# First mixer of an eight-layer stack: four moves of work and of loads around its filters

## Chip, cores and metric

The kernel runs on one core of a Trainium2 chip. The metric is device time in microseconds (us) of one execution.

## The reference

The reference is a stack of four mixers and four feed-forward layers, each as `x = x + layernorm(layer(layernorm(x)))`, on 8 sequences of 512 tokens with 256 channels in float32. Only the first mixer is touched:

```python
q, k, v = short_conv(x @ W.T, conv)                 # each with silu
beta = sigmoid(x @ Wb.T)
A = where(strictly_lower, -(kb @ k.T), 0)           # per chunk of 32 tokens; kb = k * beta
T = inverse(eye - A); u = T @ v; w = T @ kb
S, o: u_adj = u - w @ S; o = q @ S + attn @ u_adj; S = S + k.T @ u_adj     # chunk by chunk
local_s, local_m, local_l = fir(v, 3 / 15 / 63 taps)
p = softmax(gate logits)                            # five gates per head
o = p0*local_s + p1*local_m + p2*local_l + p3*delta + p4*v
out = rmsnorm(o) @ Wo.T
```

## The kernel before

`l0_attn` (from line 275) works in three stages. Instructions are written in Python order, but that is only a priority: a planner puts every instruction on its engine's list at build time, by a model of its own, and takes the first in Python order whose inputs and buffers it believes to be ready. On the chip each list then runs strictly in order, with semaphore waits. The SyncE queue (SP) issues nearly all loads and stores, ScalarE's queue (ACTq) a few stores.

**Front**, per block b of 512 tokens, 0 to 7 (`front`, lines 434 to 511): normalise and transpose x (L133 on VectorE, L146 on TensorE), project to k, q, v (L448), convolve over four taps (L454 on ScalarE, L456 on VectorE), silu (L459), transpose v into the resident tile `Vw` (L486, L488), and form the products k·k of 64-token chunks (L499, L502), stored to DRAM as `s_d` (L505, L509).

`strengths(g, p)` (L372) turns the rows of four blocks into beta over the squared norm of k and writes them to `g_d`: two loads of rows (L377), a tanh (L381), four small VectorE instructions (L382 to L386), four stores (L388). It runs after block 3 for group 0 and after block 7 for group 1, with its tiles in the front's pool.

`inverse(g)` (L328) is a generator for the chunk inverses of four blocks. It works in the residual's own tiles, `K.XA`, which are loaded again later (`K.load_x`, L74). Its first step loads 2 MB of products (L331) and the strengths (L333). Then come some 60 VectorE instructions in the tile (L343 to L357). Its tail is an `affine_select` and a small copy on GpSimd (L360, L363), one store of 2 MB (`t_d`, L364), and four ScalarE copies of 128x1024 (L367), each followed by a 512 KB store (`tt_d`, L368) and sharing two buffers `tt`. One step of `inverse(0)` is taken at each step of the front from block 4 on, tail included.

**Filters**, 32 groups g of 8 channels (`filters`, L617): TensorE multiplies `Vw` with a Toeplitz tile (L627, two PSUM tiles per group, six PSUM buffers). Three Toeplitz tiles exist, two of them in `K.XA[4:8]`; each is loaded afresh for its next group (L544, L547). VectorE multiplies by the gates (L632, two buffers `pr`) and adds the four terms (L638 into `s1`, L640 into `s2`, two buffers); ACTq stores the result to `f_d` (L642). `gates(h)` (L566 to L585) makes the gates of head h from `rw_all` (loaded by L553). `scaled_v` (L612) and `query_scales` (L590 to L599) prepare operands of the third stage. The filters' pools `fa`, `fb` reuse the memory of the front's pools.

**Back**, per block (`back`, L725): loads (`loads`, L695 to L720: `load_tt` L401, L699, L702, L705, L712 to L720), chunk products from L735 on, sequential state, residual sum (L182). Before it stand `inverse(1)`'s first step and `load_x` of blocks 0 to 3. The loop takes one step of `inverse(1)` at every second step, drains it when block 3 has begun, and then loads block 4.

Of the kernel before, what the change touches and what calls it, by code (L numbers as in the profile page):

```python
# [14 lines left out]
ALU = mybir.AluOpType  # L15
# [259 lines left out]
def l0_attn(K):  # L275
    nc, tc = K.nc, K.tc
# [4 lines left out]
    HALF = NB // 2  # L281
    with ExitStack() as es:
        def pool(stack, name, bufs, **kw):
            return stack.enter_context(tc.tile_pool(name="l0" + name, bufs=bufs, **kw))
# [15 lines left out]
        def window(t, offset, *ap):  # L300
            a = t[0:1, 0:1]
            return bass.AP(tensor=a.tensor, offset=a.offset + offset, ap=[list(x) for x in ap])
# [25 lines left out]
        def inverse(g):  # L328
            flat = K.XA[:, HALF * g:HALF * g + HALF].rearrange("p b n d -> p (b n d)")
            T = flat.rearrange("p (i j) -> p i j", i=64)  # L330
            nc.sync.dma_start(out=flat, in_=s_d[g * P:(g + 1) * P, :])  # L331
            gb = pin.tile([P, 64], F32, tag="gb", name=f"gb{g}")
            nc.sync.dma_start(  # L333
                out=gb, in_=window(g_d, g * P * 64, (64, P), (1, 64)))
            gn = pin.tile([P, 64], F32, tag="gn", name=f"gn{g}")
            nc.vector.tensor_scalar(gn, gb, -1.0, None, ALU.mult)
            yield

            def blocks(t, at, *ap):
                return bass.AP(tensor=t.tensor, offset=t.offset + at,  # L340
                               ap=[list(t.ap[0])] + [list(x) for x in ap])
            both = blocks(flat, 0, (2080, 2), (64, 32), (1, 32))
            nc.vector.tensor_tensor(  # L343
                both, both, blocks(gn, 0, (32, 2), (1, 32), (0, 32)), ALU.mult)
            yield
            for j in range(1, 31):
                r = 31 - j
                tmp = pin.tile([P, 512], F32, tag="tmp", name=f"tmp{g}_{j}")
                tmp = tmp[:, 0:2 * r * j].rearrange("p (q a b) -> p q a b", q=2, a=r)
                low = blocks(flat, 64 * (j + 1), (2080, 2), (64, r), (1, j))  # L350
                nc.vector.tensor_tensor(
                    tmp, blocks(flat, 64 * (j + 1) + j, (2080, 2), (64, r), (0, j)),
                    blocks(flat, 64 * j, (2080, 2), (0, r), (1, j)), ALU.mult)
                nc.vector.tensor_tensor(low, low, tmp, ALU.add)
                if j % 2:
                    yield
            nc.vector.tensor_tensor(  # L357
                both, both, blocks(gb, 0, (32, 2), (0, 32), (1, 32)), ALU.mult)
            yield
            nc.gpsimd.affine_select(  # L360
                out=T, in_=T, compare_op=ALU.is_gt, fill=0.0, base=0,
                pattern=[[1, 64], [-1, 64]], channel_multiplier=0)
            nc.gpsimd.tensor_copy(flat[:, 0:4096:65], gb)  # L363
            nc.sync.dma_start(out=t_d[g * P:(g + 1) * P, :], in_=flat)  # L364
            for q in range(4):
                tt = pin.tile([P, 16, 64], F32, tag="tt", name=f"tt{g}_{q}", bufs=2)
                nc.scalar.copy(tt, T[:, :, 16 * q:16 * q + 16].rearrange("p i j -> p j i"))  # L367
                nc.scalar.dma_start(  # L368
                    out=tt_d[g * P:(g + 1) * P, 1024 * q:1024 * q + 1024],
                    in_=tt.rearrange("p i j -> p (i j)"))  # L370
            yield

        def strengths(g, p):

            rw = p.tile([32, 2, 4, 64], F32, tag="rws", name=f"rws{g}")
            for m, at in enumerate((0, 28)):
                nc.sync.dma_start(  # L377
                    out=rw[:, m].rearrange("p h t -> p (h t)"),
                    in_=rows_d[32 * g:32 * g + 32, at * 64:at * 64 + 256])
            bt = p.tile([32, 256], F32, tag="bts", name=f"bts{g}")  # L380
            nc.scalar.activation(bt, rw[:, 0].rearrange("p h t -> p (h t)"), AF.Tanh, scale=0.5)  # L381
            nc.vector.tensor_scalar(bt, bt, 0.5, 0.5, ALU.mult, ALU.add)  # L382
            den = rw[:, 1].rearrange("p h t -> p (h t)")
            nc.vector.tensor_scalar(den, den, 1e-6, None, ALU.add)
            nc.vector.reciprocal(den, den)
            nc.vector.tensor_tensor(bt, bt, den, ALU.mult)  # L386
            for b in range(HALF):
                nc.sync.dma_start(  # L388
                    out=window(g_d, (HALF * g + b) * 2048, (256, NT), (1024, 2), (1, 256)),
                    in_=bt[J * b:J * b + J, :])  # L390
# [15 lines left out]
        with ExitStack() as e1:  # L406
            pv = pool(e1, "v", 1)
            Vw = pv.tile([P, NB, J, D], F32, name="Vw")
            with ExitStack() as ef:
                p1, p2, p3 = pool(ef, "a", 1), pool(ef, "b", 2), pool(ef, "d", 3)  # L410
# [100 lines left out]
                        in_=S[64:128, :, :, 0:64])  # L511

                inv = iter(())
                for b in range(NB):
                    for _ in front(b):
                        next(inv, None)
                    if b % HALF == HALF - 1:
                        strengths(b // HALF, p1)
                    if b == HALF - 1:
                        inv = inverse(0)  # L520
                        next(inv)

            with ExitStack() as ef:
                p1, p2 = pool(ef, "fa", 1), pool(ef, "fb", 2)
# [93 lines left out]
                def filters(g):  # L618

                    h = g // 8  # L620
                    pr = p2.tile([P, 4, 4, 64], F32, tag="pr", name=f"pr{g}")
                    for half in range(2):
                        ps = pmm.tile([P, 2, 4, 64], F32, tag="fir", name=f"pf{g}_{half}")
                        for m in range(2):
                            for r in range(2):
                                c = 4 * r + 2 * half + m
                                nc.tensor.matmul(  # L627
                                    ps[64 * r:64 * r + 64, m],
                                    lhsT=Vw[:, :, :, 8 * g + c].rearrange("p b j -> p (b j)"),
                                    rhs=toep[g % NB_T][:, :, :, c],  # L630
                                    start=True, stop=True)
                        nc.vector.tensor_tensor(  # L632
                            pr[:, 2 * half:2 * half + 2], ps[:, :, :, ::-1],
                            gt[:, h, None].to_broadcast([P, 2, 4, 64]), ALU.mult)
                    if g + NB_T < G:
                        load_toep(g + NB_T)
                    s1 = p1.tile([P, 4, 2, 64], F32, tag="s1", name=f"s1_{g}")
                    nc.vector.tensor_tensor(s1, pr[:, :, 0:2, :], pr[:, :, 2:4, :], ALU.add)  # L638
                    s2 = p2.tile([P, 4, 64], F32, tag="s2", name=f"s2_{g}")
                    nc.vector.tensor_tensor(s2, s1[:, :, 0, :], s1[:, :, 1, :], ALU.add)  # L640
                    for r in range(2):
                        nc.scalar.dma_start(  # L642
                            out=f_d[:, (8 * g + 4 * r) * 64:(8 * g + 4 * r + 4) * 64],
                            in_=s2[64 * r:64 * r + 64].rearrange("p c t -> p (c t)"))

                gates(0)
                given = False
                for g in range(G):
                    filters(g)
                    if g % 8 == 4 and g < 24:  # L650
                        gates(g // 8 + 1)
                    if g == 2:
                        value_scales()
                    if g == 22:
                        query_scales()
                    if g % 4 == 3:
                        scaled_v(g // 4)
                    if next(inv, 0) == 0 and not given:
                        given = True
                        for b in range(2):  # L660
                            load_tt(b)
        assert given
        inv = inverse(1)
        next(inv)
        K.load_x(K.i["x"], range(HALF))


        p1, p2 = pool(es, "ba", 1), pool(es, "bb", 2)
# [203 lines left out]
        K.log_exp_tables()  # L872
        K.log_exp = True
        ahead = {b: loads(b) for b in range(2)}
        live, done, begun, steps = [back(0, *ahead[0])], 0, 1, 0
        while live:
            for x in list(live):
# [188 lines left out]
class Choice:  # L1066
# [7 lines left out]
    E, NL, K = 48, 10, 128  # L1074
# [1556 lines left out]
```

## Time and profile before

| | |
|---|---|
| time, median of 3 runs | 4565.85 us (4554.68 to 4568.97) |
| profiled execution: time; span | 4579.0 us; 4577.3 us |
| TensorE / VectorE / ScalarE / GpSimd busy | 87% / 59% / 43% / 45% |
| first mixer in the span | 0 to about 705 us |
| its filters, TensorE continuously | 278.50 to 387.45 us |
| mean granted TensorE clock over the span | 0.925 |

The span runs from the first to the last instruction; the profiled time is 1.7 us more. A line of the timeline gives start, duration, engine, source line, operation, tile written <- tile read, shapes and count; in brackets stand the idle time before it and what ended that. A line of the waits gives the waiting instruction <- the one waited for: total us, times, longest. A row of a table by stage gives the stretch, its length, the busy time (and instructions) of TensorE, its weight loads, VectorE, ScalarE and GpSimd, then the granted TensorE clock as a share of full speed, the share of the 16 DMA engines, and GB/s.

### The profile page before, as it was taken

How to read it: one execution, taken by the hardware profiler on the slowest of the kernel's cores; microseconds unless marked ns; L12 is line 12 of the kernel's file. 1: busy time of each engine (PE TensorE's matmuls, PEld its weight loads, DVE VectorE, ACT ScalarE, POOL GpSimd, SP SyncE). 2: the span in 40 equal slices, each digit the busy share in tenths (PEclk: the TensorE clock that was granted, in tenths of full speed). 3: DMA queues.
4: the chain of work that ended last, by engine and by line, in shares of the span. 5: the costliest groups of instructions: out<-in, count | busy, mean ns of one | idle time of the engine just before them, and what ended most of it. 6: DMA issues, size and time to landing. Idle time of an engine off the chain costs nothing. (4 is left out here: it accounts for less than half of the span.)

```text
span 4577.3 us, 63200 instructions
## 1 busy us (share of the span) xinstructions
PE 3989.2 (87%) x21672; PEld 2642.3 (58%) x21672; DVE 2710.9 (59%) x7215; ACT 1982.9 (43%) x4082; POOL 2043.3 (45%) x2013
## 2 busy tenths in 40 slices
PE   8887898999998599789999978898988866899997
PEld 3435675555555399644454544565655544678884
DVE  7677656456647611255566534888888899721115
ACT  5511433444344233334444444767676655311112
POOL 0000322444344234345555423889888879223321
PEclk9897998999999799889999989999999986899999
DMA  4467621000000199500000002344333434236653
GB/s 117 142 180 193 174 50 45 18 10 6 7 5 20 52 249 251 148 5 10 6 6 6 1 23 67 122 125 127 124 123 121 125 106 138 93 121 230 228 182 113
DMA packets 389361, 442.89 MB, mean 97 GB/s; under 512 B 147469, under 2 KB 271487, under 8 KB 388527
## 3 DMA queue, kind: packets, MB, share of 16 engines
q1 hardware_dynamic: 361087, 390.18, 28.4%
q0 software_dynamic: 16272, 31.87, 2.6%
q10 hardware_dynamic: 11680, 16.80, 1.1%
q8 instruction: 172, 2.82, 0.3%
q14 instruction: 150, 1.23, 0.1%
HBM read 372.49 MB, written 66.26 MB: 96 GB/s over the span
## 5 line engine op out<-in xcount | busy, mean ns | idle before, releaser
L2046 POOL TENSOR_TENSOR h<-h,C 128x1024 f32<-128x1024 f32 x256 | 613.5, 2409 | 137.6 <-DVE h L2042 95.0
L2042 DVE TENSOR_TENSOR_SCAN h<-dA,dB 128x512 f32<-128x512 f32 x480 | 568.1, 1208 | 91.0 <-ACT dA L2030 77.3
L1000 POOL TENSOR_SCALAR p<-p,rs 128x128 f32<-128x128 f32 (+3 forms) x256 | 275.9, 1085 | 416.5 <-DVE rs L999 260.5
L2030 ACT ACTIVATE dA<-dl,A 128x512 f32<-128x512 f32 x480 | 330.5, 690 | 174.4 <-DVE h L2042 173.6
L1566 DVE CUSTOM_DVE_ANT_0 junk<-S,mask 128x256 f32<-128x256 f32 (+3 forms) x512 | 249.5, 487 | 195.1 <-PE S L1560 156.8
L2059 PE MATMUL y<-C,h 128*128 128x128 f32 x2048 | 295.3, 295 | 73.0 <-POOL h L2046 72.8
L2059 PEld LDWEIGHTS y<-C,h 128*128 128x128 f32 x2048 | 260.2, 153 | 158.5 <-POOL h L2046 102.9
L1594 ACT ACTIVATE PT<-T 128x128 f32<-128x128 f32 (+3 forms) x512 | 198.1, 435 | 278.9 <-PE T L1589 267.9
L1560 PE MATMUL S<-KZ,QT 64*128 64x512 f32 (+3 forms) x1024 | 260.1, 491 | 23.8 <-DVE mx L1566 23.6
L2258 PE MATMUL gb<-xbT,w_b 128*128 128x256 f32 (+1 forms) x1472 | 255.3, 332 | 1.0 <-ACT ts L2462 0.6
L2258 PEld LDWEIGHTS gb<-xbT,w_b 128*128 128x128 f32 x1472 | 230.2, 191 | 23.1 <-ACT ts L2462 0.8
L2264 DVE TENSOR_TENSOR hTb<-sb,gb 128x512 f32<-128x512 f32 x71 | 48.8, 687 | 325.4 <-PE gb L2258 314.1
L2025 POOL TENSOR_TENSOR dB<-du,B 128x1024 f32<-128x1024 f32 x96 | 233.8, 2436 | 0.1
L1844 PE MATMUL pf<-fT,w_l_ffn 128*128 128x512 f32 x384 | 206.6, 676 | 28.5 <-ACT fT L1838 11.3
L1589 PE MATMUL T<-QT,KZ 64*128 64x384 f32 (+3 forms) x1024 | 217.1, 465 | 2.9 <-ACT PT L1594 2.5
L2025 DVE TENSOR_TENSOR dB<-du,pb 128x1024 f32<-128x1024 f32 x160 | 191.2, 1195 | 23.4 <-ACT pb L2023 21.3
L182 POOL TENSOR_TENSOR X<-X,yn 128x256 f32<-128x256 f32 (+1 forms) x56 | 79.7, 1441 | 263.0 <-ACT yn L177 233.1
L1334 ACT ACTIVATE hT<-h,w_l_ffn 128x128 f32<-128x128 f32 x384 | 109.5, 368 | 198.0 <-PE h L1329 198.0
L1329 PE MATMUL h<-xgT,w 128*128 128x128 f32 x1536 | 185.1, 279 | 0.0
L1560 PEld LDWEIGHTS S<-KZ,QT 64*128 64x128 f32 x1024 | 116.7, 193 | 114.0 <-issue 58.3
L1597 POOL TENSOR_SCALAR_AFFINE_SELECT PT<-PT 128x512 f32<-128x512 f32 x128 | 81.3, 635 | 219.1 <-ACT PT L1594 206.2
L998 ACT ACTIVATE p<-p,nm 128x128 f32<-128x128 f32 (+3 forms) x256 | 143.5, 561 | 80.7 <-DVE nm L994 72.7
(587 smaller groups left out, 9147.0 us busy)
## 6 DMA issues: line engine op xcount, KB each, us to landing
w_b<-l3f_w SPq DMA_DIRECT2D x138, 512.0 KB
C<-xdd SPq DMA_DIRECT2D x256, 256.0 KB
B<-xdd SPq DMA_DIRECT2D x256, 256.0 KB
w<-l1f_w SPq DMA_DIRECT2D x48, 1024.0 KB
w<-l1f_w SPq DMA_DIRECT2D x48, 256.0 KB
X<-x SPq DMA_DIRECT2D x16, 512.0 KB
c<-ys SPq DMA_DIRECT2D x16, 512.0 KB
X<-l0fd SPq DMA_DIRECT2D x22, 320.0 KB
```

Source lines behind the costliest of these rows:

```text
L1000: nc.gpsimd.tensor_scalar(p[:, 0:n], p[:, 0:n], rs, None, ALU.mult)
L1560: nc.tensor.matmul(ps[:, 0:n], lhsT=QT[half, qt * P:n], rhs=KZ[half, j % 2, 0:n], start=True, stop=True)
L1566: nc.vector.tensor_tensor_reduce(out=junk[:, 0:n], in0=ps[:, 0:n], in1=mask[:, L - n:L], scale=1.0, scalar=-3.0e38, op0=ALU.add, op1=ALU.m ...
L1589: nc.tensor.matmul(ps[:, 0:n], lhsT=KZ[half, j % 2, kt * P:(kt + 1) * P], rhs=QT[half, kt * P:L], start=True, stop=True)
L1594: nc.scalar.activation(PT[:, j, :], ps[:, 0:n], AF.Exp)
L1844: nc.tensor.matmul(ps, lhsT=gu[:, k, j * 768 + c * P:j * 768 + (c + 1) * P], rhs=R[b]["fT"][:, k, :], start=(k == 0), stop=(k == 1))
L2025: on.tensor_tensor(dBs[k], R[b]["du", h], B[:, None, :].to_broadcast([P, 2, L]), ALU.mult)
L2030: nc.scalar.activation(dA, R[b]["dl", h][:, c, :], AF.Exp, scale=A[:, 2 * h + c, n:n + 1])
L2042: nc.vector.tensor_tensor_scan(hs[k][:, c, :], dA, dBs[k][:, c, :], 0.0, ALU.mult, ALU.add)
L2046: nc.gpsimd.tensor_tensor(hs[k], hs[k], row_C.pop(k)[:, None, :].to_broadcast([P, 2, L]), ALU.mult)
L2059: nc.tensor.matmul(R[b]["y", h][q // 2][:, q % 2, c * P:(c + 1) * P], lhsT=t[:, c, q * P:(q + 1) * P], rhs=K.ident, is_transpose=True, sta ...
L2258: nc.tensor.matmul(ps[:, q, :], lhsT=ww[:, k, (c + q) * P:(c + q + 1) * P], rhs=xT[:, k, :], start=(k == 0), stop=(k == 1))
```

## The change

It has four parts. The tail of `inverse(0)` is no longer stepped during the front: the step in front of it now yields `True`, at which the front stops stepping, and the tail is written after filter group 1, followed by `load_tt` of blocks 0 and 1. `strengths(1)` moves from the end of the front to filter group 21, with its tiles in the filters' pool. The two sums of the filters go from VectorE to GpSimd. And `load_x` of blocks 0 to 3 and the first step of `inverse(1)` are written after the loads of back blocks 0 and 1 instead of ahead of them, `load_x` first.

```diff
@@ inverse
             nc.vector.tensor_tensor(
                 both, both, blocks(gb, 0, (32, 2), (0, 32), (1, 32)), ALU.mult)
-            yield
+            yield True
             nc.gpsimd.affine_select(
@@ the loop over the front
                 inv = iter(())
+                inverted = True
                 for b in range(NB):
                     for _ in front(b):
-                        next(inv, None)
-                    if b % HALF == HALF - 1:
-                        strengths(b // HALF, p1)
+                        inverted = inverted or next(inv)
                     if b == HALF - 1:
+                        strengths(0, p1)
                         inv = inverse(0)
-                        next(inv)
+                        inverted = next(inv)
+                assert inverted
@@ filters
-                    nc.vector.tensor_tensor(s1, pr[:, :, 0:2, :], pr[:, :, 2:4, :], ALU.add)
+                    nc.gpsimd.tensor_tensor(s1, pr[:, :, 0:2, :], pr[:, :, 2:4, :], ALU.add)
                     s2 = p2.tile([P, 4, 64], F32, tag="s2", name=f"s2_{g}")
-                    nc.vector.tensor_tensor(s2, s1[:, :, 0, :], s1[:, :, 1, :], ALU.add)
+                    nc.gpsimd.tensor_tensor(s2, s1[:, :, 0, :], s1[:, :, 1, :], ALU.add)
@@ the loop over the filters
                 gates(0)
-                given = False
                 for g in range(G):
                     filters(g)
...
                     if g % 4 == 3:
                         scaled_v(g // 4)
-                    if next(inv, 0) == 0 and not given:
-                        given = True
+                    if g == 1:
+                        for _ in inv:
+                            pass
                         for b in range(2):
                             load_tt(b)
-        assert given
-        inv = inverse(1)
-        next(inv)
-        K.load_x(K.i["x"], range(HALF))
+                    if g == 21:
+                        strengths(1, p1)
@@ the back
         ahead = {b: loads(b) for b in range(2)}
+        K.load_x(K.i["x"], range(HALF))
+        inv = inverse(1)
+        next(inv)
         live, done, begun, steps = [back(0, *ahead[0])], 0, 1, 0
```

## The prediction, made before the changed kernel was run

> **What bounds the stage now.** The change touches only the first mixer, some 705 us of the span, so I cut that into stages and asked in each what TensorE waits for. First the table by stage: front blocks 4, 5, 6 and 7, the hand-over to the filters, the filters, the hand-over to the back.
>
> ```profile
> 122.67:147.97 25.30, 23.64 (x97) 11.19 (x97) 21.04 (x35) 15.53 (x30) 2.01 (x2) 1.00 0.63 183
> 147.97:182.42 34.45, 27.53 (x98) 13.88 (x97) 32.64 (x61) 15.97 (x29) 0.20 (x1) 0.80 0.23 57
> 182.42:220.53 38.11, 27.25 (x97) 13.84 (x97) 22.10 (x43) 23.07 (x32) 6.45 (x4) 0.84 0.51 172
> 220.53:248.84 28.31, 26.36 (x97) 12.00 (x96) 13.32 (x20) 16.73 (x30) 0.00 (x0) 0.91 0.62 159
> 248.84:278.50 29.66, 11.69 (x49) 4.95 (x49) 21.04 (x44) 2.31 (x4) 1.80 (x1) 0.74 0.87 227
> 278.50:387.45 108.95, 108.42 (x464) 47.05 (x464) 83.83 (x163) 0.94 (x2) 0.00 (x0) 0.98 0.65 194
> 387.45:402.69 15.24, 0.00 (x0) 0.03 (x1) 8.73 (x17) 1.28 (x1) 4.27 (x11) 0.57 0.78 229
> ```
>
> An undisturbed block takes 25.30 us with TensorE busy for 23.64. Block 5 is long by VectorE, which carries the inverse (32.64 of 34.45). Block 6 is longer still, 38.11, though VectorE has only 22.10: something else. The filters are TensorE's (108.42 of 108.95). Both hand-overs leave TensorE idle, 17.97 and 15.24 us. The timeline of ScalarE in block 6 and the waits of that stretch say why:
>
> ```profile
> 213.73 1.91 ACT L367 COPY tt<-X 128x1024 f32<-128x1024 f32 x1 [2.81 <-DMA l0tt<-tt]
> 215.55 0.58 ACT L488 COPY Vw<-pvw 128x512 f32<-128x512 f32 x1
> ...
> 216.04 1.95 ACT L367 COPY tt<-X 128x1024 f32<-128x1024 f32 x1
> 217.90 0.57 ACT L488 COPY Vw<-pvw 128x512 f32<-128x512 f32 x1
> ```
>
> ```profile
> DVE ca L456 <- ACT ca L454: 22.7, 1, 22.7
> ```
>
> The inverse's copies sit between the front's own, one of them waiting for a store to free its buffer, and VectorE starves for 22.7 us. Then the waits of the first hand-over, of SP at the second, and of the back:
>
> ```profile
> POOL toep L536 <- DMA l0g<-bts: 44.4, 1, 44.4
> ...
> PE pf L627 <- DVE rw_all L567: 9.8, 1, 9.8
> ...
> PE pf L627 <- DVE pr L632: 8.1, 1, 8.1
> DVE rky L90 <- DMA l0g<-bts: 5.6, 1, 5.6
> ```
>
> ```profile
> SPq L702 <- DMA l0v<-vs: 8.4, 1, 8.4
> ```
>
> ```profile
> PE pW L735 <- DMA TS<-l0t: 15.3, 1, 15.3
> ```
>
> The filters' pool opens only when the second strengths are stored (their tile is in memory that it reuses); TensorE then waits for the gates. At the other end the first back block waits for its load L702, and that for memory that the last store of `vs` still reads.
>
> **Part 1, the tail held.** In block 4 the last convolution instruction ends at 142.44 + 1.52 = 143.96, and the next block's first transpose starts at 147.97, 4.0 us later. In block 6 it ends at 201.43 + 4.02 = 205.45, and the next starts at 220.53: 15.1 us, 11.1 more. The next block's transposes to projections take 225.90 - 220.53 = 5.4 us instead of 151.42 - 147.97 = 3.5, another 1.9. At most 13.0 us go. But I don't expect the copies to wait for the filters: the list takes whatever is ready. The Toeplitz tile's memset ran at 126.91, and three residual loads, written after all filters, at 218.02. So the tail keeps its time and only loses its rank: the four copies (4 x 1.95 = 7.8 us) become fillers in ScalarE's gaps. One gap of 3.48 us per block is free; the others are about 1 us, and a copy started there delays the front by up to 1. I charge 5 of 7.8: gain 8.0, from 13.0 - 7.8 = 5.2 to 13.0 if order alone decides, and zero if the copies keep their place. Next late is TensorE itself (23.64 of 25.30). With the copies move GpSimd's 4.07 + 0.37 us (L360, L363), a 2 MB store on SP, four of 512 KB on ACTq, and behind them the `load_tt` and residual loads that wait for it. If all that were held until group 1, GpSimd's 4.4 us would stand ahead of the sums, 1.2 groups of 3.76 us, against three groups of PSUM; the transfers are rival S.
>
> The trace shows that slow clock: eight transposes took 1.97 us after the stall against 1.09 in other blocks, at a granted 0.91 for the block. [...]
>
> **Part 2, strengths at group 21.** The pool now waits for the last store of products, issued until 251.55, instead of the last store of strengths, issued until 255.76: 4.2 us. The strengths store landed 1.5 to 1.7 us after issue; the products' store is larger (256 against 8 KB), so I take 2.5 (0 to 4.2). At its new place it costs four VectorE instructions (0.28 + 0.28 + 1.74 + 0.41 = 2.7 us), beside 25 us of VectorE slack in the filters, and on SP two loads and four stores (1.22 + 3.95 us of issue) ahead of Toeplitz loads. The eight stores of L599 took 3.96 us there at 373.56 and TensorE did not stop. Without that cover the price is 5.2 us less the spare of the triple buffer. If it is taken early, its 2.7 us may stand ahead of the gates; that is inside my bound.
>
> **Part 3, sums on GpSimd.** VectorE loses 21.1 + 12.4 = 33.5 us. GpSimd has add-like 128x512 at 1.27 (L862) and 128x256 at 0.72 (L182): 1.99 us per group against TensorE's 108.95 / 29 = 3.76. It adds waits: `pr` of group g+2 now waits for GpSimd's sum of group g, and GpSimd for the store before last; six PSUM buffers lie in front. Since TensorE is busy 108.42 of 108.95, at most 0.5 us can be won, and I take 0.5. The last sums end at about 388.14 + 1.99 = 390.1 instead of 390.75, because `vs` no longer stands between.
>
> The groups of the filters, and then GpSimd's and VectorE's timelines in a back block:
>
> ```profile
> L638 DVE TENSOR_TENSOR s<-pr 128x512 f32<-128x512 f32 x31 | 21.1, 681 | 0.0
> ...
> L640 DVE TENSOR_TENSOR s<-s 128x256 f32<-128x256 f32 x30 | 12.4, 412 | 4.1 <-DMA l0f<-s 4.1
> ```
>
> ```profile
> 423.41 2.34 POOL L723 TENSOR_TENSOR bq<-bq,PQ 128x1024 f32<-128x1024 f32 x1 [11.29 <-DMA PQ<-l0pq]
> ```
>
> ```profile
> 423.45 2.81 DVE L354 TENSOR_TENSOR X<-X,tmp 128x480 f32<-128x480 f32 x1
> ```
>
> The last two lines speak against it: the same VectorE instruction takes 0.65 us alone and 2.81 beside GpSimd's. But L864, which reads one operand from PSUM, kept 0.68 beside L862. In the filters L632 reads PSUM too; only the gates, `vs` and L94 to L96 read two SBUF tensors, 21 instructions there. If each waits 1.3 us, that is 27 us, less than the 33.5 that left: covered.
>
> [...]
>
> **Part 4, block loads first.** L331's 2 MB went out at 387.45, L699 at 389.64, L702 at 398.93, and TensorE started 3.8 us after that. If L702 goes out beside L699, it starts at 393.4, 9.3 us earlier. But L331's tile is free with the last filter matmul, the block's memory perhaps later; then the list still takes L331 first, and the gain is 0. After the start the DMA engines are full (1.07 busy, 249 GB/s to 428.65), so part is lost again. I take 6 (0 to 9.3). `inverse(1)` starts later by up to 34 us: two blocks' loads of 3.1 MB and the residual's 2.1 MB at 249 GB/s. Its results are loaded for block 4 until about 516 and used at 541.5, 25 us of cover. Block 3's loads waited 26.7 us on SP for a `tt` store, and block 2 to 3 took 40.3 us against 32.4; a new order may drop or repeat that (-8 to +8), taken as 0.
>
> **Sum.** 8.0 + 2.5 + 0.5 + 6.0 = 17 us, against the profiled 4579.0: 4562. That execution lies 13 us above the median, so from 4565.85 the forecast is 4549.
>
> **Rivals.**
> *N, no effect:* ready work is taken early anyway, copies and L331 keep their places; only parts 2 and 3 count, 3 us: 4563. For it: the memset at 126.91. Against it: rank decides wherever two are ready.
> *S, slower:* the tail's store and the residual loads, 4.2 MB on SP, go out just ahead of `rw_all` and the first Toeplitz loads. At 249 GB/s they hold the gates 16.8 us. Bursts of 2 MB (8.4 us) against a spare of two groups less a load (7.5 - 2.3 = 5.2) cost another 3 x 3.2 = 9.6. Less 8.0 from the front: +18, 4584. It begins when they go out less than 16.8 us ahead of L553, and outweighs the front's gain at once if less than 8.4. For it: DMA at 0.87 in that hand-over.
> *I, inverse late:* 34 us against 20 to 25 of cover: block 4 waits 12, leaving 5: 4561.
>
> **Chances.** Forecast 0.60, N 0.16, S 0.16, I 0.08. About 0.3%, 13.7 us, can be told from no change; of the forecast's case, which spans 4522 (13.0 + 4.2 + 0.5 + 9.3 + 8 = 35, and 9 for a better clock and lists behind) to 4558, 0.45 lies beyond it and 0.15 within. Faster 0.45, same 0.15 + 0.16 + 0.08 = 0.39, slower 0.16. The range 4522 to 4578 leaves out about 0.05 below and, of S, 0.12 above.
>
> **What would show it.** Right: block 6 near 30 us; L536 before 256; the filters still 109 us; L702 before L331 and TensorE within 7 us of the last filter. Wrong: a gap inside the filters with a Toeplitz load behind a 2 MB transfer, L331 still first, or `pr` waiting for GpSimd.

## The result and the profile after

The changed kernel takes 4588.59 us (median of 6 runs, 4582.23 to 4591.94) against 4566.16 us before (6 runs, 4554.68 to 4568.97): a ratio of 1.005, 95% interval 1.0038 to 1.0061. It is about 22 us slower. The forecast, 4549 us and faster, and its range to 4578 us are both missed.

The profiled execution after took 4589.72 us. First its table by stage, in the columns of the table in the prediction: front blocks 4, 5, 6, 7, the hand-over, the filters, the second hand-over.

```profile
122.67:147.97 25.30, 23.65 (x98) 11.18 (x97) 21.05 (x35) 15.54 (x30) 2.02 (x2) 1.00 0.63 182
147.97:182.42 34.45, 27.53 (x98) 13.89 (x98) 32.63 (x60) 15.99 (x29) 0.21 (x1) 0.80 0.23 57
182.42:213.18 30.76, 25.48 (x97) 12.54 (x97) 22.10 (x43) 17.62 (x29) 6.46 (x4) 0.89 0.52 167
213.18:245.02 31.84, 27.78 (x97) 13.96 (x96) 13.14 (x20) 22.00 (x33) 0.00 (x0) 0.84 0.61 167
245.02:273.17 28.15, 11.69 (x49) 4.93 (x49) 17.96 (x40) 2.53 (x4) 1.80 (x1) 0.82 0.97 239
273.17:387.40 114.23, 108.42 (x464) 48.68 (x464) 70.32 (x108) 2.22 (x3) 67.07 (x62) 0.95 0.65 195
387.40:396.80 9.40, 0.00 (x1) 0.00 (x0) 0.69 (x1) 0.00 (x0) 6.16 (x13) 0.61 0.60 143
```

Block 6 is 30.76 us instead of 38.11, as forecast. The filters start 5.3 us earlier, but take 114.23 instead of 108.95, and end where they ended before. The second hand-over falls from 15.24 to 9.40. So the back starts 5.6 us early (block 0's copy in the table of milestones below), and yet the first mixer ends 16 us late. The waits of TensorE from 240 to 400 us, and SP's issues and TensorE's timeline inside the filters (both cut), show the lost 5.3 us:

```profile
PE pW L734 <- DMA TS<-l0t: 9.7, 1, 9.7
PE pf L628 <- DVE rw_all L571: 8.5, 1, 8.5
PE pf L628 <- DVE pr L633: 7.9, 1, 7.9
PE pf L628 <- DMA toep<-l0fd: 5.8, 1, 5.8
```

```profile
345.07 4.56 SPq L388 DMA_DIRECT2D l0g<-bts  x4
...
354.37 6.11 SPq L600 DMA_DIRECT2D l0pq<-rqy  x8
360.58 0.34 SPq L545 DMA_DIRECT2D toep<-l0fd  x1
```

```profile
351.38 7.64 PE L628 MATMUL pf<-X,Vw 128*64 128x256 f32 x32
364.84 3.98 PE L628 MATMUL pf<-toep,Vw 128*64 128x256 f32 x16 [5.81 <-DMA toep<-l0fd]
```

The four stores of the strengths and the eight of the query scales (L600; L599 before) now stand close together, ahead of a Toeplitz load, and TensorE stops for 5.81 us.

The larger loss is in the back. I take as milestones the copies of `W` by ScalarE (L740 before, L739 after), the first product of each back block:

| block | 0 | 1 | 2 | 3 | 4 | 5 | 6 | 7 |
|---|---|---|---|---|---|---|---|---|
| before, us | 404.65 | 431.37 | 470.20 | 510.48 | 542.07 | 574.44 | 606.83 | 639.20 |
| after, us | 399.05 | 418.57 | 452.01 | 501.45 | 554.30 | 591.30 | 623.50 | 655.21 |
| difference | -5.6 | -12.8 | -18.2 | -9.0 | +12.2 | +16.9 | +16.7 | +16.0 |

At block 2 the changed kernel is 18.2 us ahead of the profile before; by block 4 it is 12.2 behind. Its table between these copies (blocks 1 to 2, 2 to 3, 3 to 4, 4 to 5; the last row is the stretch from block 0's copy to block 7's):

```profile
418.57:452.01 33.44, 29.46 (x381) 23.32 (x381) 21.50 (x54) 10.24 (x22) 3.49 (x3) 0.98 0.97 230
452.01:501.45 49.44, 43.78 (x378) 34.44 (x378) 40.16 (x74) 11.43 (x24) 11.14 (x6) 0.67 0.25 70
501.45:554.30 52.85, 44.19 (x409) 34.74 (x410) 31.47 (x97) 23.79 (x39) 14.87 (x8) 0.74 0.64 178
554.30:591.30 37.00, 32.41 (x357) 25.80 (x358) 19.02 (x55) 9.40 (x19) 6.36 (x5) 0.77 0.61 143
399.05:655.21 256.16, 223.79 (x2555) 178.85 (x2556) 152.03 (x373) 84.89 (x164) 56.34 (x32) 0.83 0.56 140
```

Between the copies of blocks 2 and 3, VectorE is busy for 40.16 of 49.44 us and TensorE for 43.78; the granted clock is 0.67 there, then 0.74 and 0.77. Over the same stretch of the profile before:

```profile
404.65:639.20 234.55, 205.34 (x2555) 164.52 (x2556) 147.62 (x361) 84.63 (x164) 57.03 (x32) 0.89 0.61 146
```

The same 2555 matmuls keep TensorE busy for 223.79 instead of 205.34 us. That is 18.5 of the 21.6 us by which the stretch grew; TensorE's idle time in it grew by only 3.2. From 400 to 660 us no wait of TensorE for a transfer is left, and its longest single wait is 3.0 us, so no block waits there for late loads. What VectorE does there besides the blocks' own work is the second inverse. Its first and last large instruction, before and after:

```profile
396.92 2.29 DVE L343 TENSOR_TENSOR X<-X,gn 128x2048 f32<-128x2048 f32 x1 [6.17 <-DMA X<-l0s]
473.55 2.28 DVE L357 TENSOR_TENSOR X<-X,gb 128x2048 f32<-128x2048 f32 x1
```

```profile
440.29 2.28 DVE L343 TENSOR_TENSOR X<-X,gn 128x2048 f32<-128x2048 f32 x1
509.88 2.29 DVE L357 TENSOR_TENSOR X<-X,gb 128x2048 f32<-128x2048 f32 x1
```

Its 2 MB load L331 stands on SP behind the loads of blocks 0 and 1 (issued at 411.57 instead of 387.45), and its VectorE work starts 43 us and ends 36 us later. It moves from beside blocks 0 and 1 to beside blocks 1 to 3, most of it beside block 2. The order of VectorE's own list says the same. VectorE, too, makes one copy of `W` per block (L741 before, L740 after): of the inverse's 62 VectorE instructions, 12 stood ahead of block 0's copy, then 23, 25 and 2 between the following copies; after the change it is 0, 0, 15, 41 and 6.

The six runs of the kernel before differ among themselves by up to 14 us. Of two profiled executions of it, one has a stretch of half clock in the back, 27.31 us from 427.15 on, that the other lacks (last section), and the profile before is the one that has it.

### The profile page after: what moved, and what is told of

Same layout as the page of the kernel before. It is cut to its first block, busy times and chain, and to the rows that moved or that the text cites. A ratio compares the mean times of both kernels' runs of the same rounds, so it can differ in the third digit from the quotient of the medians.

```text
span 4588.0 us, 63259 instructions
## 1 busy us (share of the span) xinstructions
PE 4002.5 (87%) x21672; PEld 2655.4 (58%) x21672; DVE 2692.9 (59%) x7151; ACT 1982.6 (43%) x4082; POOL 2115.0 (46%) x2077
## 5 line engine op out<-in xcount | busy, mean ns | idle before, releaser
L2497 POOL DMA_INDIRECT ys<-yb,place x71 | 70.1, 987 | 239.2 <-ACT yb L2496 225.0
```

## Theories and experiments

Theory L, the forecast's own rival I: the second inverse ends late and block 4 waits for its results. Theory C: nobody waits for it; its VectorE work beside blocks 2 and 3 stretches them, and TensorE spends them at half clock. Theory O: the order of the loads on SP's queue itself costs the time. And the parts could simply add up, each with its own small loss. "Half clock" below is the time with a granted clock under 0.75, in slices of half a microsecond from 380 to 700 us. It was 72.5 us in the profile before and 98.5 us after. All differences are medians against runs of the kernel before on the same chip; intervals are of the ratio.

### Each part alone

**Tail alone.** The front and filter edits of part one, with strengths still at the end of the front.

```diff
-                        next(inv, None)
+                        inverted = inverted or next(inv)
...
-                    if next(inv, 0) == 0 and not given:
-                        given = True
+                    if g == 1:
+                        for _ in inv:
+                            pass
                         for b in range(2):
                             load_tt(b)
```

> Only the tail of the first inverse is moved behind filter group 1; strengths, sums and block loads stay as before. Theory (the loss is in the block loads' order): the trace after the change shows the next transposes of block 7 7.4 us earlier, but three of the four copies still lie in block 7, which is 3.5 us longer, so the filters' first matmul should come about 4 us earlier and the end of the first mixer 2 to 6 us earlier: time -2 to -6 us against before. Rival (the tail's store and the residual loads collide with the filters' loads): a gap of TensorE behind a 2 MB transfer inside the filters or before them, time +5 to +15 us.

Measured: +2.5 us, ratio 1.0009 (1.0 to 1.0018); neither the expected gain nor the rival's loss. Block 7's transposes start at 211.33 instead of 220.53, 9.2 us earlier, but the filters run continuously only from 276.55 instead of 278.50: TensorE waits 15.5 us for the gates instead of 9.8, as the filters' pool opens at 256.32 instead of 257.48, hardly earlier. So most of the front's gain is not passed on while part two is missing.

**Strengths alone.**

```diff
-                    if b % HALF == HALF - 1:
-                        strengths(b // HALF, p1)
                     if b == HALF - 1:
+                        strengths(0, p1)
...
+                    if g == 21:
+                        strengths(1, p1)
```

> Only the second strengths are moved to filter group 21; all else as before. Theory: the filters' pool opens 3 to 5 us earlier, and the loads and four stores on SP near the end of the filters stand ahead of Toeplitz loads; the combined change showed a gap of 5.8 us there. Alone, the eight stores of the query scales need not fall together with the four of the strengths, so a gap of 0 to 6 us is expected and a time of -4 to +2 us against before. Rival (these stores carry the loss): +10 us or more, with a gap in the filters of 10 us.

Measured: -5.2 us, ratio 0.999 (0.9981 to 0.9998), somewhat more than expected. The filters run from 276.05 instead of 278.50, and there is no gap behind a Toeplitz load.

**Sums alone.**

```diff
-                    nc.vector.tensor_tensor(s1, pr[:, :, 0:2, :], pr[:, :, 2:4, :], ALU.add)
+                    nc.gpsimd.tensor_tensor(s1, pr[:, :, 0:2, :], pr[:, :, 2:4, :], ALU.add)
```

(and the same for `s2`)

> Only the two sums of the filters go to GpSimd. Theory: TensorE sets the filters' length, so -2 to +2 us against before, with the filters' stretch still 109 us. Rival (VectorE and GpSimd slow each other, or the product buffers come free late): waits of VectorE's gate product for GpSimd's sums, filters 5 us or more longer, time +5 us or more.

Measured: +5.2 us, ratio 1.001 (0.9999 to 1.002). That is outside what I expected, though not proven slower, and its profile has one new wait of TensorE in the filters and its place on SP:

```profile
PE pf L627 <- DMA toep<-l0fd: 5.4, 1, 5.4
```

```profile
353.48 8.64 SPq L599 DMA_DIRECT2D l0pq<-rqy  x8
364.94 0.34 SPq L544 DMA_DIRECT2D toep<-l0fd  x1
```

With VectorE relieved, the planner's list makes the query scales 20 us earlier, and their stores stand ahead of six pairs of Toeplitz loads instead of one. The strengths are at their old place in this kernel, so the gap belongs to this part. I see no cost of the sums themselves: in the filters of the changed kernel (the groups of that stretch) VectorE's product waited for GpSimd's sum for 2.0 us in all, before 280 us.

```profile
L639 POOL TENSOR_TENSOR s<-pr 128x512 f32<-128x512 f32 x32 | 44.3, 1384 | 62.0 <-DVE pr L633 37.6 <-DMA X<-x 19.9 <-DMA l0f<-s 3.8
L633 DVE TENSOR_TENSOR pr<-pf,gt 128x512 f32<-128x512 f32 x64 | 43.4, 687 | 43.8 <-PE pf L628 41.7 <-POOL s L639 2.0
```

**Loads alone.**

```diff
-        inv = inverse(1)
-        next(inv)
-        K.load_x(K.i["x"], range(HALF))
...
         ahead = {b: loads(b) for b in range(2)}
+        K.load_x(K.i["x"], range(HALF))
+        inv = inverse(1)
+        next(inv)
```

> Only the order at the end of the filters is changed: loads of back blocks 0 and 1 first, then the residual's loads and the first step of the second inverse. Theory (the late inverse carries the loss): the store of products' load goes out 24 us later and the inverse's 60 VectorE instructions move from beside blocks 0 and 1, which wait for transfers anyway, to beside blocks 2 and 3; blocks 0 to 2 run 10 to 20 us ahead and then lose 30 to 35, so the end of the first mixer is 14 to 26 us later and the time +14 to +26 us. Rival (the forecast's: early block loads win): -6 us, block 2 early and block 4 not late. Second rival (the loss needs the other parts): within 5 us of before.

Measured: -1.4 us, ratio 0.9995 (0.9985 to 1.0005): no effect to be told. My expectation of +14 to +26 fell. The written order changed, but SP's built list did not: L331 still stands ahead of all block loads, and the inverse's instructions lie 12, 23, 25, 2 as before. The four parts alone sum to +1.1 us, the change to +22: an interaction.

### Which parts together

> The change with its fourth part undone: residual loads and the second inverse's first step ahead of the block loads again. The single parts gave +2.5, -5.2, +5.2 and -1.4 us against before, together +1, while all four give +22. In the single fourth part SP's list still has the inverse's load L331 ahead of all block loads; only where the sums are on GpSimd too does it fall behind the loads of blocks 0 and 1. Theory (the loss is L331 behind the block loads, which needs parts three and four together): this kernel has L331 first and comes out at the sum of the single parts, -4 to +6 us against before. Rival (the parts add up, or the loss is in the gap that strengths and query scales open in the filters): near +20 us.

```diff
+        inv = inverse(1)
+        next(inv)
+        K.load_x(K.i["x"], range(HALF))
...
         ahead = {b: loads(b) for b in range(2)}
-        K.load_x(K.i["x"], range(HALF))
-        inv = inverse(1)
-        next(inv)
```

The change without its part four: +0.7 us, ratio 0.9998 (0.9989 to 1.0008). L331 is first again, the inverse lies 12, 23, 25, 2, half clock 54.0 us. The gap behind the Toeplitz load is there (6.3 us), and the filters run from 269.48: together, tail and strengths (here beside the sums) bring 9 us at the filters' start, where alone they brought 2.0 and 2.5.

> Parts three and four alone: sums on GpSimd and block loads first. Theory: L331 falls behind the loads of blocks 0 and 1, the second inverse starts some 40 us late, and the time is +20 to +32 us against before, with blocks 3 and 4 of the back late as in the full change. Rival (single parts add): +4 us. Second rival (the loss needs the strengths' stores or the held tail): within 6 us of before.

Its edit is the two diffs of "sums alone" and "loads alone" on the kernel before. Parts three and four alone: ratio 1.0068 (1.0055 to 1.0082), +31.7 us. The inverse lies 0, 0, 15, 41, 6; half clock 95.0 us. The additive rival (+4) falls. Part four puts the block loads first only where the sums are on GpSimd. My reading is that the planner then believes the block loads' memory to be free before the tile of L331, which no run shows.

> The change with its third part undone: the sums stay on VectorE. Theory: L331 is first in SP's list again, no gap of 5 us in the filters, and the single gains of tail, strengths and loads add to -4 us (-10 to +2) against before. Rival (lateness comes from the written order, not from the sums): +15 to +25 us.

```diff
-                    nc.gpsimd.tensor_tensor(s1, pr[:, :, 0:2, :], pr[:, :, 2:4, :], ALU.add)
+                    nc.vector.tensor_tensor(s1, pr[:, :, 0:2, :], pr[:, :, 2:4, :], ALU.add)
...
-                    nc.gpsimd.tensor_tensor(s2, s1[:, :, 0, :], s1[:, :, 1, :], ALU.add)
+                    nc.vector.tensor_tensor(s2, s1[:, :, 0, :], s1[:, :, 1, :], ALU.add)
```

The change without part three: ratio 0.9989 (0.998 to 0.9999), -4.1 us, as expected. L331 is first, there is no gap in the filters, and they run from 269.96.

> The change, but with the second inverse's first step written between the loads of block 0 and those of block 1, and the residual's loads last. L331 then stands behind one block's loads instead of two. Theory (lateness of the inverse is the price): L331 goes out some 10 us later than before instead of 24, within the lead that the early loads give, so the time is -6 to +6 us against before; the loss isn't half of +22 but nearly gone. Rival (any load ahead of L331 costs in proportion): +8 to +14 us.

```diff
-        ahead = {b: loads(b) for b in range(2)}
-        K.load_x(K.i["x"], range(HALF))
+        ahead = {0: loads(0)}
         inv = inverse(1)
         next(inv)
+        ahead[1] = loads(1)
+        K.load_x(K.i["x"], range(HALF))
```

Ratio 1.005 (1.0038 to 1.0062), +22.5 us: my expectation fell, and the proportional rival too. L331 went out at 396.39, 9 us later than before, but shared the DMA engines with block 0's loads (share 1.04 until the inverse began), and the inverse began on VectorE at 418.30. Its instructions lie 0, 13, 33, 16; half clock 92.0 us. A delay of 21 us cost as much as one of 43. So the price is not the delay itself.

### Results late, or work in the wrong place?

In the first kernel nothing depends on the second inverse's results; in the second, half of its elimination steps are left out.

> The change, but back blocks 4 to 7 load the inverses of blocks 0 to 3 instead of their own, so that nothing waits for the second inverse; it still runs in full beside blocks 1 to 4. The output of these four blocks is not the reference's. Theory L (block 4 waits for results that come too late, as in the forecast's rival): the loss goes, block 4's first copy comes near 530 us instead of 554, time 0 to +5 us against before. Theory C (the inverse's VectorE work and the half clock that follows it stretch blocks 2 to 4, whoever uses the results): block 4 stays at 545 us or later, half-clock time of TensorE in the back stays above 85 us, and the time stays at +15 to +24 us.

```diff
-                    in_=window(tt_d, (b * 32 + r * 16) * 4096,
+                    in_=window(tt_d, (b % HALF * 32 + r * 16) * 4096,
...
-                in_=window(t_d, (b * 32 + 16) * 4096, (64, 32), (4096, NT * H), (1, 32)))
+                in_=window(t_d, (b % HALF * 32 + 16) * 4096, (64, 32), (4096, NT * H), (1, 32)))
...
-                in_=window(t_d, b * 32 * 4096, (64, 64), (4096, NT * H), (1, 64)))
+                in_=window(t_d, b % HALF * 32 * 4096, (64, 64), (4096, NT * H), (1, 64)))
```

Ratio 1.0057 (1.0044 to 1.0071), +28.2 us. With nobody waiting for the second inverse's results, the loss stays whole, block 4's copy comes at 551.39 and the half clock is 106.0 us. As in the changed kernel, TensorE waits for no transfer from 400 to 660 us. Theory L is out. Its blocks 2 to 3 and 3 to 4:

```profile
455.80:502.17 46.37, 40.71 (x378) 31.75 (x378) 39.88 (x72) 11.44 (x23) 11.16 (x6) 0.72 0.27 53
502.17:551.39 49.22, 41.59 (x383) 31.87 (x384) 29.41 (x95) 20.40 (x32) 10.25 (x6) 0.69 0.57 181
```

> The change, but the second inverse does only the odd one of its 30 elimination steps: half of its small VectorE instructions, some 17 of 35 us, are left out, and its results are wrong for blocks 4 to 7. Load, first and last steps, copies, stores and loads stay. Theory C: with half of the work beside blocks 2 and 3 VectorE has room, TensorE's half-clock time in the back falls from 98 us to about 60, and the time to between -8 and +5 us against before. Rival (a fixed loss from the order of the loads on SP's queue, such as block 4's loads waiting behind the inverse's tail): still +12 us or more, with the half-clock time near 90 us.

```diff
-            for j in range(1, 31):
+            for j in range(1, 31, 1 + g):
```

Ratio 0.9999 (0.999 to 1.0008), -1.3 us: with half of the steps left out the loss is gone, though L331 is as late as in the change. Half clock 64.5 us. From its block 3's copy to block 4's the clock is 1.00. (With fewer steps the inverse also ends earlier, at 476.5 instead of 512.2 us, and its copies and stores follow earlier.) Blocks 2 to 3 and 3 to 4:

```profile
451.81:495.25 43.44, 36.88 (x367) 29.84 (x368) 31.10 (x66) 19.51 (x29) 15.52 (x8) 0.67 0.34 120
495.25:530.18 34.93, 32.19 (x395) 26.12 (x396) 22.83 (x70) 12.53 (x27) 8.20 (x5) 1.00 1.02 236
```

Three more kernels start from the kernel before and hold the second inverse's VectorE work by a real dependence on a back block's attention; `(b, n)` is (0, 1), (0, 3) and (1, 0). L331 stays first on SP, and the loads of blocks 0 to 3 keep their order; the inverse's tail and the loads of block 4 follow the held work. Once released, the inverse is stepped at every step of the loop instead of every second:

```diff
                 nc.vector.tensor_tensor(oT[:, :, tok], F[:, :, tok], po, ALU.add)
+                if (b, n) == (0, 3):
+                    neg.append(p1.tile([P, 1], F32, name="neg"))
+                    nc.vector.tensor_scalar(neg[0], oT[:, 0, tok][:, 0:1], 0.0, -1.0, ALU.mult, ALU.add)
...
+            yield
             gn = pin.tile([P, 64], F32, tag="gn", name=f"gn{g}")
-            nc.vector.tensor_scalar(gn, gb, -1.0, None, ALU.mult)
-            yield
+            nc.vector.tensor_scalar(gn, gb, neg[0] if g else -1.0, None, ALU.mult)
...
-            if steps % 2:
+            if neg:
                 next(inv, None)
```

> The kernel before, with its load L331 first, but the second inverse's first VectorE instruction takes its constant from block 0's second attention chunk, so that VectorE's list has none of the inverse's 62 instructions ahead of block 1's first copy, 34 between those of blocks 1 and 2, and 28 between 2 and 3 (before: 12 ahead of block 0's, then 23, 25, 2; after: 0, 0, 15, 41, 6). Theory C (the place of the VectorE work makes the loss): +6 to +18 us against before, less than after's +22. Rival (the order of the loads on SP's queue is needed): within 4 us of before.

> As j_late01, but held until block 0's last attention chunk: 24 of the inverse's instructions between the copies of blocks 1 and 2, 38 between 2 and 3, which is nearest to after's 0, 0, 15, 41, 6. Theory C: +14 to +26 us against before, with TensorE at half clock for 85 us or more in the back. Rival: within 4 us of before, half clock 48 to 72 us.

> As j_late01, but held until block 1's first attention chunk: 37 between the copies of blocks 2 and 3, 25 between 3 and 4. Theory C: +15 us or more; and here block 4 could wait for the results on top, +25 to +40. Rival: within 4 us of before.

Ratios 1.007 (1.0057 to 1.0083), 1.0072 (1.0058 to 1.0086), 1.0083 (1.007 to 1.0096): +31.6, +31.3 and +36.5 us, half clock 105.5, 88.0 and 98.5 us. The first two lost more than I expected. In the third, block 4 does wait for its results, so its loss is a mixture:

```profile
PE pW L737 <- DMA TS<-l0t: 15.9, 1, 15.9
```

The first two have no such wait in blocks 1 to 7. Theory O is out as a condition: holding the inverse's work makes a loss of this size with L331 first and the block loads in their order. The inverse's tail (GpSimd, ScalarE's copies, stores) moved with the held work, and no run moves the one without the other. Two of the kernels above speak against the tail as the cause: with half of the steps left out it began 25 us after block 2's copy of `W`, with L331 halfway 26 us after it, and the first lost nothing, the second 22.5 us. In the second held kernel, blocks 2 to 3 and 3 to 4 look like the change's:

```profile
458.26:509.30 51.04, 40.00 (x382) 31.37 (x382) 41.91 (x92) 12.23 (x27) 11.05 (x6) 0.77 0.25 68
509.30:566.33 57.03, 46.02 (x409) 35.38 (x410) 32.45 (x82) 23.74 (x39) 14.97 (x8) 0.70 0.70 192
```

### Controls and a faster version

> The kernel before once more, as a control for the size of differences and for a profile from the same chip as the others. All theories: 0 us, at most 0.1% either way; in its back L331 ahead of the block loads and about 70 us of half clock.

Ratio 1.0001 (0.9991 to 1.0012) for this control. Its profiled execution's block 7 copies `W` at 625.21, not 639.20, with 48.0 us of half clock instead of 72.5 and of the 70 that I expected.

> The change without its third part (the version that took -4.6 us against before), with one addition: the value scales take their constant from a finished gate, so that they and the scaled values can't stand ahead of the gates on VectorE. In that version VectorE spent 253.0 - 248.1 us on the value scales, then two scaled values, and waited 3.6 us for a store of them, with the gates behind it and TensorE waiting 9.5 + 8.1 us. Expected: TensorE starts the filters in earnest 6 to 10 us earlier, and the time falls to -8 to -14 us against before. Rival (the transfers of the first Toeplitz tiles and of the gates' rows are late anyway): within 3 us of -4.6.

```diff
-                    nc.vector.tensor_scalar(sk, sk, 1e-6, None, ALU.add)
+                    e6 = p1.tile([P, 1], F32, name="e6")
+                    nc.vector.tensor_scalar(e6, gt[:, 0, 3, 0:1], 0.0, 1e-6, ALU.mult, ALU.add)
+                    nc.vector.tensor_scalar(sk, sk, e6, None, ALU.add)
```

The change without part three, and with this: ratio 0.9973 (0.9962 to 0.9984), 4553.1 against 4564.64 us, -11.5 us, 7 more than without the addition. It beats both kernels. The second wait of TensorE in the hand-over shrinks from 8.12 to 3.34 us, and the filters run from 265.78 instead of 269.96, 4.2 us earlier where I expected 6 to 10 (timeline):

```profile
258.46 3.98 PE L631 MATMUL pf<-toep,Vw 128*64 128x256 f32 x16 [8.60 <-DVE wgm L573]
265.78 7.68 PE L631 MATMUL pf<-X,Vw 128*64 128x256 f32 x32 [3.34 <-DVE pr L636]
```

> The kernel before with only the addition that keeps the value scales behind the gates. In the version with tail and strengths moved it took some 7 us more off. Expected alone: -4 to -8 us, the filters starting 5 to 7 us earlier. Rival (the filters' pool, which opens at 257 us here, is what is late): within 2 us of before.

The same addition to the kernel before: ratio 1.0 (0.9991 to 1.001), no effect to be told, although its filters run from 274.97 instead of 278.50. So the gates' place pays only with tail and strengths moved. Where the 3.5 us are lost again, the runs don't show.

## Why the prediction was wrong

**Step that failed: part 4, "Its results are loaded for block 4 until about 516 and used at 541.5, 25 us of cover."** The delay was sized rightly for the load (24 us; "up to 34") and too low for the work on VectorE (43 us). But cover was counted for the results, and the results are not what costs: with nobody waiting for them the change lost 28 us. What I put at nothing was the inverse's own work in its new place, L351 and L354, 17.2 + 17.5 us of VectorE in the back, most of which now lies beside block 2. In the kernel before that work lay beside blocks 0 and 1, and there it cost little: in the control, at a clock of 1.00, the stretch from block 1's copy to block 2's took 28.38 us with 14.8 us of the inverse in it (its row is in the last section), and in the third held kernel, where the inverse had not begun, the same stretch took 26.35:

```profile
426.47:452.82 26.35, 24.44 (x353) 19.77 (x354) 14.19 (x34) 9.81 (x20) 3.49 (x3) 1.00 0.96 209
```

In the new place TensorE ran slowly (in the change, a clock of 0.67 between the copies of blocks 2 and 3). The second held kernel, with L331 first and no block waiting for results, lost 31 us.

**The 6 us of part 4** were right as a local size: the hand-over shrank by 5.8 us, and blocks 1 and 2 came 12.8 and 18.2 us early. All was given back from block 2 on. And by itself the part does not do what it says: alone it left L331 first, the 0 end of my term. Its sign was decided by part 3, which I had held to be separate. **The sum of separate terms** is the second step that failed: tail and strengths together brought 8.5 to 9.0 us at the filters' start (with the sums on VectorE and on GpSimd) against 2.0 and 2.5 alone, and parts 3 and 4 together lost 31.7 us against +5.2 and -1.4.

**Part 1, 8.0 us:** of this 7.4 us were won at block 7's transposes in the change, and 9.2 with the tail alone. The copies did become fillers, three of them in block 7 (at 215.05, 216.90 and 222.23). At the end of block 7 the change without part four, with the same copies, was 7.5 us early, close to my term; block 7 took 28.35 us at a clock of 1.00. In the changed kernel it took 31.84 at 0.84, and 3.8 us were left. So a slow clock did come back, but not at the next transposes: these ran fast (1.10 us), and matmuls slowed from 232.57 us on (1.92 us for two that had taken 1.04, the granted clock at 0.50 from 232.50), behind idle times of 1.22 and 0.71 us. With the tail alone the same two pairs kept 1.05 us each, behind 1.21 and 0.71 us.

**Part 2, 2.5 us:** alone, the filters started 2.5 us earlier, but the number is luck. The pool opened at 255.79 instead of 257.48, 1.7 us, and by the trace it waited for a Toeplitz load, not for the products' store; the rest came from shorter waits for the gates. The time fell by 5.2 (interval -9 to -1). The cover "TensorE did not stop" held alone. The 5.8 us stop in the change is not due to the strengths' stores alone: with the sums on GpSimd and the strengths at their old place it was 5.4, behind the query scales' stores.

**Part 3, 0.5 us and covered:** some of VectorE's instructions were longer beside GpSimd's sums, and the filters were not. Two of three L94 at 128x256 took 1.38 us, each begun while a sum ran on GpSimd (from 333.87 and 337.58 us); the third, begun between two sums, took 0.41, as all three did before. The product that reads PSUM took 0.687 against 0.685. Without the 5.81 us stop the filters are as long as before (108.42 of 108.95). The cost came from the lists: stores earlier in the filters, and L331 later.

**The correction by 13 us** to the median was right in direction, and has a likely cause. The profile before and the control's profile lie 19.7 us apart, and 14.0 us of that at block 7's copy. The former has 24.5 us more half clock, which at half speed would be some 12 us, an estimate.

**Rivals.** Rival I named the right agent, the late inverse, with the wrong mechanism and 0.08 of chance. S expected a slower kernel and a gap in the filters. The gap came, but behind small stores on SP, not behind 2 MB transfers, and it is not the loss: the change without part four has it too and loses nothing.

**The clock's share.** From block 0 to block 7, TensorE's busy time grew by 18.5 us against the profile before (31.9 against the control) of 21.6 (36.2) in all, with as many matmuls. In the rows of that stretch the granted clock is 0.83 of 256.16 us after, 0.89 of 234.55 before and 0.96 of 220.00 in the control, so the clock lost 43.5, 25.8 and 8.8 us of full speed. The control's row:

```profile
405.21:625.21 220.00, 191.89 (x2555) 153.71 (x2556) 147.01 (x361) 84.69 (x165) 57.04 (x32) 0.96 0.65 156
```

By this estimate the clock lost 18 us more after the change than in the profile before (35 more than in the control), about as much as TensorE's busy time grew. So most of the loss is TensorE running slowly, with the caution that its records have modelled ends.

What is not settled is how the inverse's VectorE work and the half clock hang together. With half of its steps left out the half clock fell from 98.5 to 64.5 us; with the work held in the kernel before it was 105.5, 88.0 and 98.5 us (control: 48.0). Beside block 1 the control shows that work at a clock of 1.00, for some 2 us. Beside blocks 2 and 3 no run held the clock up under the same VectorE load.

## What to carry over

Before moving a load that feeds a side job, look at where that job's instructions will run, not only at when its results are needed: here a job of 35 us on VectorE cost some 2 us where 15 us of it lay beside one block and the clock stayed up, and 22 to 32 us in all once it stood mostly beside later blocks, where TensorE spent more time at half clock (88 to 106 us, against 72.5 and 48 in the two profiles of the kernel before). Where a planner lays the lists, compare the built lists before summing terms; an edit that seems to touch only one engine can reorder another engine's queue, and a "reordering" can leave the list as it was. Price small stores on a queue by what stands behind them: here a Toeplitz load, and TensorE stopped for 5.81 us.

## What the hardware showed beyond expectation

In the backs of the profiles here the granted clock of TensorE falls to 0.50 for stretches that I read as 3.5, 6.5 to 7, 10, 17, 20.5, 24, 27.5 and 31 us, in readings of half a microsecond. In the changed kernel's trace the stretches at 0.50 that begin at 450.95, 491.91, 505.57, 532.87 and 560.18 us last 27.31, 6.83, 20.48, 6.83 and 17.07 us: 8, 2, 6, 2 and 5 times the 3.41 us of the shortest in that trace (from 41.35 us on). In the 3.41 us ahead of each of these five falls TensorE's records fill 1.19, 0.68, 1.40, 1.42 and 1.35 us, so none was wholly idle. In the first of the five the clock was at 0.50 although TensorE's records fill every slice inside it but one (2.33 of 3.00 us from 471.00 to 474.00). After the change (3 us each; the clock is the third number from the end):

```profile
447.00:450.00 3.00, 0.78 (x10) 0.54 (x11) 2.94 (x12) 0.50 (x2) 0.00 (x0) 1.00 0.58 224
450.00:453.00 3.00, 3.00 (x73) 2.81 (x73) 2.40 (x9) 1.38 (x3) 0.00 (x0) 0.66 0.03 8
453.00:456.00 3.00, 3.00 (x15) 2.67 (x14) 2.90 (x5) 1.91 (x5) 1.38 (x1) 0.50 0.00 0
...
474.00:477.00 3.00, 3.00 (x22) 2.77 (x22) 1.73 (x4) 0.00 (x0) 0.00 (x0) 0.50 0.09 14
477.00:480.00 3.00, 3.00 (x27) 2.69 (x26) 0.95 (x3) 0.61 (x2) 0.76 (x1) 0.79 0.45 167
```

In the first slice VectorE is busy for 2.94 of 3.00 us, with the inverse's instructions between a block's own, and TensorE waits for VectorE's copy of the state:

```profile
449.76 0.71 PE L809 MATMUL pr<-state,bk 128*128 128x128 f32 x4 [2.22 <-DVE state L834]
```

This wait of 2.22 us ends at 449.76, and the 27.31 us of half clock begin at 450.95. What makes the clock fall and return no run here shows, and in one and the same kernel it falls or doesn't: blocks 1 to 2 of the kernel before, in the profile before and in the control.

```profile
431.37:470.20 38.83, 36.75 (x354) 29.02 (x354) 24.61 (x54) 9.31 (x18) 3.65 (x3) 0.66 0.45 97
```

```profile
427.72:456.10 28.38, 25.25 (x354) 19.79 (x354) 25.98 (x58) 9.32 (x19) 3.65 (x3) 1.00 0.85 164
```

The same 354 matmuls on the same list take 36.75 us of TensorE at 0.66 and 25.25 at 1.00. A single profiled execution of such a stage is not enough to size a change of 10 us.
